# A new written order for the beginning of a two-layer cross-attention kernel: the second pair's context loaded and cast early, all values ahead of the first scores of group 1

## The chip, the cores and the metric

The kernel runs on one core of a Trainium2 chip. The metric is the device time of one execution in microseconds. Of the kernel before, three runs were timed: 1496.53, 1501.82 and 1505.2 us, median 1501.82. One further execution was profiled and took 1496.42 us.

## The reference

Two cross-attention layers follow each other over x, 16 sequences of 256 tokens and 320 channels, with a context of 16 x 256 tokens and 512 channels. There are 20 heads of 16 channels. Layer 0 takes the first 77 context tokens as text and the other 179 as image tokens; layer 1 takes the last 4 as image tokens. In short, for layer 0:

```
q, k, v   = x @ Wq, text @ Wk, text @ Wv          (k_ip, v_ip from the image tokens)
text_out  = softmax(q k / 4) v                    per head
text_probs= softmax((q . k_text over all channels) / 4)
sem       = (text_probs @ text) . image / 4       one number per query and image token
ip_out    = softmax(q k_ip / 4 + sem / 2) * spatial_mask @ v_ip
x         = (text_out + ip_out) @ Wout + bout + x
```

Layer 1 has the same shape, with the semantic part per head and normalised. All is float32.

## The kernel before

**Precision.** Most products are made of float32r parts: a tensor is cast to a high half on ScalarE (`nc.scalar.copy`), and its low half is the difference, made on VectorE or POOL (`tensor_sub`). `cast(hi, lo, src)` (L231) issues the ScalarE part at once and returns a function that issues the low half on a given engine (L237); `halves` (L157, L160) does both. A product is then hi*hi + hi*lo + lo*hi.

**Layer 0.** Work goes by sequence b and by group g of four heads: 5 groups a sequence, 80 slots of layer 0, then 80 of layer 1. Sequences are taken in pairs c for the context: `keys0(c)` loads four context blocks of 128 channels x 512 tokens (256 KB each), casts them, and makes six key products, text and image for each of three blocks m of 128 key rows (the third has 64). Keys and queries go out to device memory and come back as stacks of heads (`stacks0`: parts K, Q, T, M), with rows appended for the semantic term and for the maxima. `values0_(b)` makes the values of one sequence in three steps of 12 matmuls (L246 by way of `prod`). `semantic0` makes the text probabilities, `tokens0` the token products M.

**A slot.** `slot0(k)` makes, in this order, the transposed maxima of group k+1 (`maxima0`, L694 to L699: two matmuls, a copy to `mt`, two small DMAs into the query stack), the plain scores of group k+2 for their maxima (`score0`, L686, reduced on VectorE at L687 and L688; it holds the one tile `whole`, two banks), the transposed scores and exponentials of its own group (`turned0`, L711 to L717), and the attention of the group before (`attend0`, L754). Between these, `fill` runs background steps: keys, queries, semantic parts, values, output products. Each background task has a list of times in slots; `fill(now)` runs all steps whose time has come, earliest first. `FIRST["k0"]` is this list for the second pair's keys: step 1 loads, steps 2 to 5 cast one block each, steps 6 to 11 are the six key products.

**Order.** TensorE runs in written order everywhere. In `begin` and `end` the other engines and their queues do too. In the slots between, a planner orders them by its own model of time, and `queued` and `anchor` add order dependencies (no semaphores) that keep a background instruction behind the slot's own on its engine. Each engine runs its instructions strictly in the order that results.

**The beginning (`begin`).** It does by hand what the tasks do later, for the first pair: it clears tiles, loads contexts, weights and the first two x, makes the text keys as blocks arrive (`key_terms`, L1416) with a few matmuls without use between them (`warm`, L730), then queries of sequence 0 (L1472), image keys, semantic parts, values of sequences 0 and 1, and the scores of groups 0 and 1. Raw loads lie in tiles that are used later for something else: `craw` (context) in the two `rawc` and the two `raw` tiles, `wkr` and `wkir` (key weights) in the four `P` tiles, `wvir` (image value weights) in `craw` again. The context tiles `ct` of pair 0 are the tiles that pair 1 takes next, so pair 1's casts come only after the last value and token product of pair 0. In slot 0 and its second half seven further `warm` matmuls each stand.

Lines that the prediction names: L83 any load or store issued by SP; L246 and L256 products of keys, values and tokens (L256 the third key block); L552 and L555 query and output projections; L541 and L542 low halves of x on POOL; L608 to L615 semantic scores; L786 and L765 transposes.

## Time and profile before

| what | us |
|---|---|
| profiled execution | 1496.42 |
| its span, first to last instruction | 1494.6 |
| TensorE busy | 1426.0 (95%) |
| TensorE weight loads | 1148.6 (77%) |
| POOL busy | 1215.5 (81%) |
| VectorE busy | 1118.7 (75%) |
| ScalarE busy | 920.2 (62%) |
| slot 0 starts | 52.05 |
| slot 1, slot 2, slot 3 start | 58.05, 73.52, 85.92 |

The start of slot 0 is that of its plain scores (L686), the starts of the others those of their transposed maxima (L694) on TensorE. The times are counted from the first instruction. Matmuls are pipelined and their ends are modelled, so a row's end can lie a little behind the start of the next. The granted clock is that of TensorE: 1.00 is the full one, and 0.50 occurs. A row of the engines' timeline has start, length, engine and line, operation, tiles out<-in, shapes, count, and in brackets the idle time of the engine in front of it with what ended it. "ACTq" and "SPq" rows are DMA issues by ScalarE's and SP's sequencers.

### The profile page before, as it was taken

How to read it: one execution, taken by the hardware profiler on the slowest of the kernel's cores; microseconds unless marked ns; L12 is line 12 of the kernel's file. 1: busy time of each engine (PE TensorE's matmuls, PEld its weight loads, DVE VectorE, ACT ScalarE, POOL GpSimd, SP SyncE). 2: the span in 40 equal slices, each digit the busy share in tenths (PEclk: the TensorE clock that was granted, in tenths of full speed). 3: DMA queues.
4: the chain of work that ended last, by engine and by line, in shares of the span. 5: the costliest groups of instructions: out<-in, count | busy, mean ns of one | idle time of the engine just before them, and what ended most of it. 6: DMA issues, size and time to landing. Idle time of an engine off the chain costs nothing.

```text
span 1494.6 us, 36273 instructions
## 1 busy us (share of the span) xinstructions
PE 1426.0 (95%) x12738; PEld 1148.6 (77%) x12738; DVE 1118.7 (75%) x2527; ACT 920.2 (62%) x2174; POOL 1215.5 (81%) x1589
## 2 busy tenths in 40 slices
PE   8999999999999989789999999999999999999998
PEld 6877888888888877577777777777777777777765
DVE  6476767676777688767777887778777877787886
ACT  5455555556565655546676676667666766676663
POOL 6379898989898978788687888888888888888785
PEclk9999999999999999889999999999999999999999
DMA  7758676767677766575434434444444344433401
GB/s 246 226 178 239 173 230 192 215 197 223 198 218 204 205 191 176 157 221 166 132 94 120 141 117 116 120 142 117 112 127 140 113 121 128 138 109 93 122 26 47
DMA packets 228673, 232.83 MB, mean 156 GB/s; under 512 B 38346, under 2 KB 198380, under 8 KB 228492
## 3 DMA queue, kind: packets, MB, share of 16 engines
q1 hardware_dynamic: 226284, 229.21, 53.4%
q8 instruction: 102, 1.67, 0.5%
q10 hardware_dynamic: 2208, 1.30, 0.4%
q14 instruction: 79, 0.65, 0.1%
HBM read 117.65 MB, written 77.07 MB: 130 GB/s over the span
## 4 chain that ended last, share of the span: by engine, by line
PE 67%; DVE 9%; POOL 9%; DMA 8%; ACT 4%; issue 3%; SPq 1%; ACTq 1%; DVEq 0%; POOLq 0%
PE X L896 13%; PE X L246 12%; PE X L552 6%; PE P L754 5%; PE S L686 5%; PE P L908 4%; PE P L918 4%; PE T L711 3%; POOL wt L887 3%; PE T L846 3%; PE S L852 3%; POOL P L717 2%; PE X L555 2%; PE X L256 2%; PE X L511 2%
## 5 line engine op out<-in xcount | busy, mean ns | idle before, releaser
L717 POOL TENSOR_TENSOR P<-P,rs 128x512 f32<-128x512 f32 x320 | 406.6, 1293 | 87.7 <-ACT P L714 86.0
L887 POOL TENSOR_TENSOR wt<-P,ctb 128x512 f32<-128x512 f32 x316 | 400.5, 1289 | 50.6 <-ACT ctb L886 50.6
L896 PE MATMUL X<-ctb,gm 128*128 128x512 f32 x1106 | 298.3, 401 | 2.6 <-DVE wt L897 2.6
L714 ACT ACTIVATE P<-T 128x512 f32<-128x512 f32 x320 | 176.0, 594 | 139.8 <-PE T L711 104.4
L897 DVE TENSOR_TENSOR wt<-X,wt 128x512 f32<-128x512 f32 x320 | 216.9, 681 | 57.6 <-PE X L896 52.4
L866 ACT ACTIVATE P<-T 128x512 f32<-128x512 f32 x320 | 174.4, 592 | 81.1 <-PE T L846 77.3
L896 PEld LDWEIGHTS X<-ctb,gm 128*128 128x128 f32 x1106 | 192.2, 189 | 41.2 <-DVE wt L897 12.1
L854 DVE TENSOR_REDUCE mn<-S 128x4 fp32r<-128x1008 f32 x160 | 191.1, 1195 | 0.0
L886 ACT ACTIVATE ctb<-P 128x512 fp32r<-128x512 f32 x316 | 181.1, 625 | 9.0 <-PE X L896 6.1
L688 DVE TENSOR_REDUCE mn<-S 128x4 fp32r<-128x716 f32 x160 | 142.4, 890 | 0.0
L754 PE MATMUL P<-P,vr 128*32 128x256 f32 x1920 | 124.8, 388 | 2.0 <-POOL P L717 2.0
L686 PE MATMUL S<-ks,qs 125*128 125x256 f32 x640 | 116.3, 304 | 5.8 <-DMA ks<-kd 2.6
L686 PEld LDWEIGHTS S<-ks,qs 125*128 125x128 f32 x640 | 87.4, 192 | 40.2 <-issue 26.8
L711 PE MATMUL T<-qs,ks 127*128 127x256 f32 x640 | 105.6, 287 | 1.2 <-ACT P L714 0.9
L687 DVE TENSOR_REDUCE mn<-S 128x4 fp32r<-128x308 f32 x160 | 74.6, 466 | 25.0 <-PE S L686 23.7
L711 PEld LDWEIGHTS T<-qs,ks 127*128 127x128 f32 x640 | 89.2, 192 | 3.1 <-ACT P L714 1.9
L754 PEld LDWEIGHTS P<-P,vr 128*32 128x32 f32 x1920 | 55.6, 111 | 43.1 <-POOL P L717 4.3
L765 DVE STREAM_TRANSPOSE nt<-P 128x512 f32<-128x512 f32 x80 | 56.8, 710 | 42.2 <-PE P L754 40.9
L918 PE MATMUL P<-wt,zone 128*32 128x256 f32 x1280 | 85.4, 379 | 0.6 <-DVE wt L897 0.6
L908 PE MATMUL P<-P,v1t 128*32 128x256 f32 x1280 | 85.7, 385 | 0.0
L246 PE MATMUL X<-wC,cta 128*128 128x324 f32 (+1 forms) x480 | 79.7, 313 | 0.3 <-DVE kst L268 0.3
L846 PEld LDWEIGHTS T<-qs,ks 50*128 50x128 f32 x640 | 49.3, 185 | 39.3 <-issue 30.5
(382 smaller groups left out, 3042.3 us busy)
## 6 DMA issues: line engine op xcount, KB each, us to landing
qd<-q SPq DMA_DIRECT2D x96, 256.0 KB
qs<-tph SPq DMA_DIRECT2D x64, 308.0 KB
rawc<-in_cT_dram SPq DMA_DIRECT2D x60, 256.0 KB
qs<-qd SPq DMA_DIRECT2D x80, 192.0 KB
ks<-kd SPq DMA_DIRECT2D x80, 192.0 KB
ks<-kd SPq DMA_DIRECT2D x160, 96.0 KB
qs<-qd SPq DMA_DIRECT2D x160, 96.0 KB
kd<-kst SPq DMA_DIRECT2D x57, 256.0 KB
```

Of the source, the lines that this page charges most:

```text
L246: last = mm(out, lhs(a, k), rhs(b, k), start=i == 0, stop=i == len(terms) - 1)
L686: mm(sp[:, h], Q[: XROW + T0, h, t * 128 : (t + 1) * 128], K[: XROW + T0, h], start=True, stop=True)
L711: mm(st[p][:, j], K[:KS0, 2 * p + j, t * 128 : (t + 1) * 128], Q[:KS0, 2 * p + j], start=True, stop=True)
L714: exp = anchor(nc.scalar.activation(pt, st[p], AF.Exp, scale=SCALE))
L717: anchor(nc.gpsimd.tensor_mul(pt, pt, rs[:, t : t + 1].to_broadcast([128, 2, S])))
L754: mm(pv[32 * s : 32 * s + 32, o : o + S], v[:, vt, h : h + 32], P[k, s // 2][:, t, s % 2], start=vt < 2, stop=vt != 1,)
L854: anchor(nc.vector.tensor_reduce(maxes[k + 2][:, t], sp[:, :, :T1], axis=AX.X, op=ALU.max))
L866: anchor(nc.scalar.activation(P[k, u][:, t], st[u], AF.Exp, scale=SCALE))
L886: nc.scalar.activation(R[k, u][:, t], P[k, u][:, t], AF.Copy, scale=0.5)
L887: anchor(nc.gpsimd.tensor_sub(W[k, u][:, t], P[k, u][:, t], f(R[k, u][:, t])))
L896: mm(yp, gm[:, gb], R[k, u][:, kt], start=i == 0, stop=i == len(blocks[n]) - 1)
L897: w1["wt"] = nc.vector.tensor_mul(W[k, u][:, n], yp, W[k, u][:, n])
```

## The change

In `begin`:
- the loads of `wk` go out on ScalarE's DMA queue, `tmask` is loaded after x0, and the copy of the identity stands behind these;
- the three value tiles are cleared on POOL, behind its other clears, and the six additions of `tmask` to their ones column are ScalarE activations later on;
- low halves of the key weights and of all three query weight blocks are made on VectorE, those of the image key weights all on POOL, their four casts together;
- the image value weights are loaded into the `P` tiles instead of `craw`, so `craw` is free after the text keys, and the second pair's context is loaded into it at once (`step(("k0", 1))`);
- all of `v0` (three steps) stands ahead of `score0(0, 0)`, all of `v1` around `score0(0, 1)` and ahead of `score0(1, 0)`; the four casts of the second pair's context (`parts(k1, ...)`) stand around the two halves of `score0(1, ...)`;
- the two calls of `maxima0` issue their DMAs from ScalarE, their default, instead of SP;
- step 5 of sequence 1's queries stands after the last image value weights.

The times of the second pair's six key products change from 1.2, 1.6, 1.6, 2, 2.2, 2.6 to 0.2, 0.6, 1, 1.2, 1.6, 2 slots. In `begin`, `queued` adds no dependency.

```diff
-    anchors = {}
+    anchors, written = {}, [True]
     def queued(inst, *behind):
+        if written:
+            return inst
...
-    FIRST = {"k0": [-1, 0.2, 0.6, 0.6, 1, 1.2, 1.6, 1.6, 2, 2.2, 2.6], "s0": [-1, -1, -1, -1, -1, 0.2, 0.6]}
+    FIRST = {"k0": [-1, -1, -1, -1, -1, 0.2, 0.6, 1, 1.2, 1.6, 2], "s0": [-1, -1, -1, -1, -1, 0.2, 0.6]}
...
-        nc.scalar.copy(ident_r, ident)
...
-        dma(tmask, tmask_d)
         for k in range(4):
             dma(craw[k], cT_d[k * 128 : (k + 1) * 128, : 2 * S])
-            dma(wkr[k], rows(wk0_d, k))
+            nc.scalar.dma_start(wkr[k], rows(wk0_d, k))
         dma(x0, by_tile(xT_d[0]))
+        dma(tmask, tmask_d)
+        nc.scalar.copy(ident_r, ident)
...
-        for v in vr:
-            V.memset(v, 0.0)
-            V.memset(vcols(v, V0W)[:, 2, :, 16], 1.0)
-            for t in range(2):
-                V.tensor_scalar_add(vcols(v, V0W)[:, t, :, 16], vcols(v, V0W)[:, t, :, 16], tmask[:, t : t + 1])
...
             P.memset(f(ks[i])[:, :, :T0], 0.0)
+        for v in vr:
+            P.memset(v, 0.0)
+            P.memset(vcols(v, V0W)[:, 2, :, 16], 1.0)
...
             low(V)
-            loww(P)
+            loww(V)
...
+        wvir = [b[:, :320] for b in both]
         for k in range(4):
-            wvir = craw[k][:, :320]
-            dma(wvir, rows(wvi0_d, k))
+            dma(wvir[k], rows(wvi0_d, k))
...
-        lowq[0](V)
-        lowq[2](P)
+        for v in vr:
+            for t in range(2):
+                to = vcols(v, V0W)[:, t, :, 16]
+                nc.scalar.activation(to, to, AF.Identity, bias=tmask[:, t : t + 1])
+        for low in lowq:
+            low(V)
         V.tensor_scalar_mul(wqt[:, 2, CH : 2 * CH], f(wqt[:, 2, CH : 2 * CH]), tmask[:, 3:4])
-        lowq[1](V)
         dma(nts[0][:, :320], rows(wv0_d, 3))
+        step(("k0", 1))
...
+        lowi = []
         for m in range(3):
             key_evac(0, m, text[m])
+        for k in range(4):
+            lowi.append(cast(*rounded(wkit[k]), wkir[k]))
+        lowi[0](P)
+        lowi[1](P)
+        for m in range(3):
             n = 64 if m == 2 else 128
             P.tensor_copy(kt[:n, m, :, :, :T0], f(kst[m][:n, :, :, :T0]))
-        lowi = [cast(*rounded(wkit[k]), wkir[k]) for k in range(2)]
-        lowi[0](V)
-        lowi[1](P)
+        lowi[2](P)
+        lowi[3](P)
...
         lowi[0](V)
         lowi[1](P)
-        parts(q1)
...
         lowi[0](V)
         lowi[1](P)
+        parts(q1)
         get(*m1)
-        v0 = ("v0", 0)
-        parts(v0)
+        v0, k1 = ("v0", 0), ("k0", 1)
+        get(*v0)
         score0(0, 0)
...
-        parts(v0)
+        parts(v1)
         score0(0, 1)
+        get(*q1)
+        parts(v1, v1)
+        maxima0(0)
         stacks0(2)
-        get(*v0)
-        get(*q1)
-        maxima0(0, nc.sync)
+        get(*v1)
         parts(s1, s1, s1)
-        parts(v1)
+        parts(k1, k1)
         score0(1, 0)
-        parts(v1)
+        parts(k1)
         score0(1, 1)
         stacks0(3)
-        get(*v1)
-        maxima0(1, nc.sync)
-        parts(s1, s1, ("k0", 1))
+        parts(k1)
+        maxima0(1)
+        parts(s1, s1)
```

More of the change, by code (lines that the diff above doesn't have):

```diff
@@ L1483, in begin @@
             key_terms(1, m, 0, image_keys[m])
-        lowi = [cast(*rounded(wkit[k]), wkir[k]) for k in range(2, 4)]
-        lowi[0](P)
-        lowi[1](P)
         qd = dram.tile([3, CH, S], F32, tag="qd0", name="qd0", bufs=2)
@@ L1531, in begin @@
         lowv[1](P)
-        lowi = [cast(wvit[k // 2][:, 0, k % 2], wvit[k // 2][:, 1, k % 2], craw[k][:, :320]) for k in range(2)]
+        lowi = [cast(wvit[k // 2][:, 0, k % 2], wvit[k // 2][:, 1, k % 2], wvir[k]) for k in range(2)]
         stacks0(1, "QTK")
@@ L1542, in begin @@
             results[s0] = e.value
-        lowi = [cast(wvit[k // 2][:, 0, k % 2], wvit[k // 2][:, 1, k % 2], craw[k][:, :320]) for k in range(2, 4)]
+        lowi = [cast(wvit[k // 2][:, 0, k % 2], wvit[k // 2][:, 1, k % 2], wvir[k]) for k in range(2, 4)]
         lowi[0](V)
         lowi[1](P)
+        parts(q1)
         get(*m1)
-        v0 = ("v0", 0)
-        parts(v0)
+        v0, k1 = ("v0", 0), ("k0", 1)
+        get(*v0)
         score0(0, 0)
@@ L1574, in xattn2 @@
         begin()
+        written.clear()
     with tc.manual_schedule(engines=PINNED):
```

## The prediction

> **What bounds the kernel now.** I read three views in this order: busy time by stretches of the first 86 us, the chain of work that ended last, then the engines' timelines at each place where the chain changes engine. The stretches are cut where the stages change: text keys of the first pair; queries, semantic part and image keys; the stretch to the first scores (L686); from there to slot 0; and slots 0, 1 and 2. Columns after the length are busy us of PE, PEld, DVE, ACT and POOL, granted clock, DMA share, GB/s.
>
> ```profile
> 0.00:16.30 16.30, 12.45 (x50) 9.39 (x51) 11.59 (x31) 8.68 (x18) 10.95 (x30) 0.81 0.86 285
> 16.30:30.20 13.90, 13.14 (x95) 12.29 (x94) 7.85 (x24) 9.63 (x31) 8.41 (x17) 0.98 0.70 216
> 30.20:37.38 7.18, 4.39 (x34) 3.96 (x34) 3.35 (x9) 3.96 (x12) 3.83 (x6) 1.00 0.79 217
> 37.38:52.05 14.67, 14.12 (x93) 13.84 (x93) 6.38 (x14) 3.35 (x10) 0.00 (x0) 0.88 0.84 250
> 52.05:58.05 6.00, 6.00 (x36) 5.20 (x37) 3.21 (x8) 4.23 (x13) 3.83 (x3) 1.00 0.81 224
> 58.05:73.52 15.47, 12.52 (x101) 10.75 (x98) 8.54 (x16) 7.16 (x16) 9.64 (x11) 1.00 0.71 197
> 73.52:85.92 12.40, 10.70 (x97) 9.44 (x95) 9.68 (x22) 6.26 (x16) 6.08 (x6) 1.00 0.73 229
> ```
>
> TensorE is busy for nearly all of 37.38 to 58.05; the loose stretches are the start, 30.20 to 37.38, and slot 1 (2.95 us idle of 15.47). All that the change can win in its own stretch lies in these 86 us; the rest of the program keeps its written order. The chain (start, us, what) says why:
>
> ```profile
> 7.19 1.09 DVE cta L237
> ...
> 30.65 3.10 DMA kd<-ho
> 33.88 3.37 DMA ks<-kd
> 37.38 1.20 PE S L686 x4
> ...
> 49.13 0.48 PE S L686 x4
> 49.60 1.77 PE X L246 x12
> ```
>
> The first low half (L237) starts at 7.19 because VectorE clears the value tiles first; the first scores wait for keys that go out to memory and back (3.10 + 3.37 us); from there TensorE runs through values of 1.77 us each, with the scores between them.
>
> **The start: memsets off VectorE, key weights on ScalarE's queue.**
>
> ```profile
> 2.00 0.95 DVE L1399 MEMSET vr<- 128x1068 f32 x1 [0.17 <-issue]
> ...
> 12.59 0.74 DVE L237 TENSOR_TENSOR wE<-nt,wE 128x260 fp32r<-128x260 f32 x3
> ```
> ```profile
> 1.82 1.25 POOL L1407 MEMSET ks<- 128x308 f32 x4
> ```
> ```profile
> 4.53 0.62 ACT L231 CAST cta<-rawc 128x512 fp32r<-128x512 f32 x1 [2.21 <-DMA rawc<-in_cT_dram]
> ...
> 9.31 0.62 ACT L231 CAST ctb<-craw 128x512 fp32r<-128x512 f32 x1 [0.18 <-DMA craw<-in_cT_dram]
> ```
> ```profile
> 11.00:12.00 1.00, 1.00 (x4) 0.81 (x4) 0.40 (x1) 1.00 (x3) 1.00 (x3) 0.50 1.08 399
> ...
> 18.00:19.00 1.00, 1.00 (x11) 1.00 (x10) 1.00 (x2) 0.00 (x0) 1.00 (x2) 1.00 0.27 87
> ```
>
> Three memsets of 0.95 us leave VectorE and become POOL's: at the 1.25/4 us that POOL takes for 308 columns, 1068 columns are about 1.08 us each, so POOL is done near 6.5 us and waits for nothing but the later image weights. The low half of block 0 can follow its cast at about 5.1 instead of 7.19: 2.1 us. Against this VectorE now also makes the low halves of the key weights (0.74 a block, four blocks), and the four blocks still arrive as before, the last cast at 9.31: its two low halves (0.69 by the row of L160 below, and 0.74) end near 11.4, and TensorE ends the text keys near 13 to 14 instead of 16.29. The DMA engines are full here (share 1.08 at 399 GB/s), so a second issuing queue brings little; four issues ahead of ScalarE's first cast take what the earlier start gives. I take 2.0 us earlier for everything up to the image keys, between 0 (the stream of loads and VectorE decide) and 3.3.
>
> The early load of the second pair's context, four times 256 KB, or 2.6 us at 399 GB/s, stands in SP's queue behind the last value weights and ahead of the query stores. Its cover is the hole at 18 to 20 us (share 0.27 at 18). Without that cover it costs up to 2.6 us on the query store and then on the keys, which is a rival below. I take 0. The six additions that move to ScalarE as activations, tmask's later place and the separate tiles for the image value weights come out as 0 by the same rows: ScalarE is idle for 7.6 of the first 16.30 us.
>
> **From the image keys to slot 0.**
>
> ```profile
> 33.54 1.22 POOL L237 TENSOR_TENSOR wD<-craw,wD 128x320 fp32r<-128x320 f32 x1 [0.89 <-ACT wD L231]
> ```
> ```profile
> 44.77 0.24 DVE L611 TENSOR_TENSOR sp<-sp,X 128x77 f32<-128x77 f32 x1 [1.59 <-ACT sp L610]
> ...
> 45.98 0.15 DVE L615 TENSOR_SCALAR mx<-mx 128x1 f32<-128x1 f32 x1
> 47.40 0.48 DVE L687 TENSOR_REDUCE mn<-S 128x4 fp32r<-128x308 f32 x1 [1.26 <-PE S L686]
> 47.79 0.89 DVE L688 TENSOR_REDUCE mn<-S 128x4 fp32r<-128x716 f32 x1
> ...
> 62.36 0.69 DVE L160 TENSOR_TENSOR ctb<-raw,ctb 128x512 fp32r<-128x512 f32 x1
> ```
> ```profile
> 43.99 0.35 ACT L696 CAST mt<-X 8x256 fp32r<-8x256 f32 x1
> ```
> ```profile
> 63.66 1.85 ACTq L699 DMA_DIRECT2D qs<-mt  x2
> ```
>
> "All values ahead of slot 0" was so already; what is new is that they all come ahead of score (1,0), three of them ahead of score (0,0). The last low half that these need (wD) ends at 34.76 now and at 32.8 then; two values of 1.77 follow, and score (0,0) can start at 36.3, with its keys landed at about 35.3. So 2.6 us of idle in front of L686 are filled, and with them the half clock that follows: 0.88 over 14.67 us is 1.76 us of lost clock. Then 0.48 + 1.77 + 0.48 + 2 x 1.77 bring TensorE to 42.6 with nothing left to lay over what comes next, which is the same work as before in a worse order. The maxima's copy starts at 42.8. From it to the first small addition of the semantic part it is 0.78 us (43.99 to 44.77); now the pair of maxima DMAs stands between them on ScalarE, 1.85 us, because they are issued there and not on SP. Queued behind them on ScalarE are the semantic copies and all four casts; VectorE waits for these. So the small additions start at 45.4 and end 1.36 later (44.77 to 46.13), at 46.8; two low halves of 0.69 follow, to 48.2; only then comes the reduction of score (1,0), 1.28 for its two parts, to 49.5. Score (1,1) has to wait for it, since there is one bank pair for plain scores. One more low half and the next reduction bring 51.4, the transposed maxima 51.6, and slot 0 starts at 51.7 instead of 52.05: **-0.35 us**. Of the 2.0 at the start, the 2.6 and the 1.76, some 6 us go into this tail, in which TensorE waits 4.8 us from 44.7 to 49.5. If ScalarE and VectorE got to the reductions at once, slot 0 would start at 45.2 (-6.8); if the start gains nothing, at 53.7 (+1.65).
>
> After such a wait the clock is low again. 2.58 us of idle cost 1.76 us in the stretch from 37.38; here part of the half-clocked time lies over the second wait, so I put half of it on slot 0: **+0.9**, between 0 and 3.4.
>
> **Slots 0 to 2.** Six key products move forward: three into slot 0, one stays in slot 1, the last two come there from slot 2.
>
> ```profile
> 59.18 0.58 PE L246 MATMUL X<-cta,wA 128*128 128x156 f32 x4
> ...
> 63.10 0.45 PE L246 MATMUL X<-ctb,wA 128*128 128x156 f32 x2 [0.39 <-DVE ctb L160]
> ...
> 70.52 1.19 PE L552 MATMUL X<-hq,wE 128*128 128x256 f32 x7 [0.96 <-POOL hq L541]
> ```
> ```profile
> 82.46 0.76 PE L246 MATMUL X<-cta 128*77 128x192 f32 x6 [1.36 <-DVE q L160]
> ```
> ```profile
> 71.72 1.97 PE X L246 x12
> ...
> 74.81 0.86 PE X L256 x8
> ```
>
> An image product is 1.97, a text product 1.29 (0.86 for 8 matmuls, 12 of them); the last block has 0.86 and 1.31. Slot 0 gets 1.29 + 1.97 + 1.29 = **+4.55**, and its warm-up matmuls stay, so nothing there hides them. Slot 1 loses these 4.55 and the waits inside the first product (63.55 - 59.18 - 1.29 = 3.08) and gets 0.86 + 1.31 = 2.17. But the query product then comes too early: it is held until POOL's low half hq, 3.26 of products plus 0.96 of wait now, 4.22; with 0.86 of products ahead the wait is 3.36, 2.40 more. Slot 1: **-3.06**. Slot 2 loses 2.17 and perhaps its wait of 1.36, since one bank fewer is in the ring there; I take half, **-2.87**, between -0.8 (the work only covered a wait) and -3.5. The three: -1.38.
>
> The sum: -0.35 + 0.9 - 1.38 = -0.8 us. The profiled execution took 1496.42, so 1495.6; it lies 5.4 under the median of the runs shown, which puts the forecast at 1501.0 as a median.
>
> A rule of the Trainium skill bears on the clock term (TensorE: Matmul & The Clock Gate, section "What's actually happening"): the half clock is the default, and only about 3.4 us of sustained activity releases it. The trace agrees as far as it goes, with 0.88 behind a wait of 2.58; by the rule the term would be nearer 3.4 than 0.9, if slot 0 has to earn a whole busy window.
>
> **The rivals.**
> - *The tail is hidden.* ScalarE gets its casts done in the waits before 42 us, or the reductions go first; then -6.8, no clock term, -1.38: 1493.6. For it: ScalarE is busy 3.35 of 14.67 us there. Against: each engine works in its written order, and the casts overwrite the context tiles that the last value still reads. Chance 0.22.
> - *The early load pushes the keys* (the one on the slower side). If the 1 MB has no hole, query stores and keys leave 2.6 us later than now: first scores at 40.0 instead of 36.3 (+3.7), plus a half-clocked stretch of 1.76. With -0.8 that is +4.7: 1506.5. It decides once keys land after 36.3. For it: 399 GB/s in the stream until 18. Against: 87 GB/s just behind it. Chance 0.14.
> - *The clock.* Slot 0 runs through two half-clocked stretches like the one behind 37.38 (1.76 us each) instead of half of one: 3.5 for 0.9, +2.6, 1503.6. For it: the wait is nearly twice that of 2.58. Against: the second wait takes part of it. Chance 0.10.
> - *The order far behind is redrawn.* From slot 0 on, the engines other than TensorE are ordered by a planner, and a shift at the start can change that order. Single waits of this kind stand late in layer 0:
>
> ```profile
> PE X L694 <- DVE mn L688: 10.9, 10, 4.9
> PE X L627 <- ACT sp L623: 6.3, 1, 6.3
> ```
>
> One more or less of both (4.9 + 6.3) is -11 or +11: 1490 or 1512. Chance 0.12, both ways alike.
>
> **How the numbers follow.** The forecast holds 0.42, with its own range 1497 to 1505. Its bounds together with the hidden tail and the early load give 1493 to 1507; to leave no more than 2 in 10 outside I add part of the redrawn order and the 0.6% by which the runs shown differ: 1487 to 1511. About 0.5%, 7.5 us, can be told from no change. Faster by more: 0.15 of the hidden tail, 0.06 of the order, 0.04 of the forecast, 0.25. Slower by more: 0.06 of the early load, 0.03 of the clock, 0.06 of the order, 0.01 of the forecast, 0.16. The rest, 0.59, is no change.
>
> **What would show it.** Right: the first low half near 5, text keys ending near 13 to 14, score (0,0) with no wait in front near 36, then one long TensorE wait in front of score (1,1), ended by VectorE's reduction, and slot 0 near 51.7; in slot 1 no waits inside key products but over 3 us in front of L552 for hq. Wrong: slot 0 before 47; L686 still waiting for ks; a slot 1 of 15 us; or a first 86 us that shortens by what the total does not show.

## The result, and the profile after

The changed kernel takes 1511.68 us (median of 6 runs, 1508.18 to 1518.67), the kernel before 1499.07 us beside it (6 runs, 1492.34 to 1505.2). The ratio is 1.0089, with a 95% interval of 1.0067 to 1.0111: 0.9% slower. The prediction was 1501.0 us and no change; 1511.68 lies just above the range, which ended at 1511. The profiled execution took 1508.18 us with a span of 1506.3, so 11.7 us more span than before. Of all executions timed below, one was slow (of y4, 2215.67 us at a granted clock of 0.556), and the ratios leave it out.

Busy time by stretches of the changed kernel, cut at the same events as before, except that the fourth stretch begins at 37.96 us, 0.47 us behind the start of the first scores (columns after the length: busy us of PE, PEld, DVE, ACT and POOL, granted clock, DMA share, GB/s):

```profile
0.00:15.26 15.26, 13.38 (x50) 10.27 (x51) 9.28 (x33) 9.85 (x24) 5.66 (x20) 1.00 0.91 310
15.26:28.90 13.64, 12.92 (x96) 12.04 (x93) 6.49 (x22) 9.72 (x32) 9.62 (x20) 1.00 0.85 265
28.90:37.96 9.06, 8.20 (x61) 7.97 (x62) 3.41 (x8) 4.94 (x13) 3.77 (x6) 1.00 0.78 227
37.96:58.17 20.21, 9.53 (x68) 8.79 (x66) 8.31 (x18) 4.16 (x10) 0.00 (x0) 0.76 0.86 236
58.17:70.57 12.40, 12.40 (x74) 11.48 (x73) 4.29 (x10) 5.43 (x15) 5.66 (x6) 0.83 0.15 39
70.57:84.69 14.12, 11.13 (x81) 9.63 (x81) 5.80 (x13) 4.91 (x12) 8.16 (x9) 0.81 0.62 206
84.69:96.19 11.50, 9.00 (x80) 7.87 (x79) 9.41 (x19) 5.36 (x13) 5.78 (x5) 0.94 0.56 142
```

| event | before, us | after, us | difference |
|---|---|---|---|
| text keys done | 16.29 | 15.26 | -1.0 |
| first scores (`score0(0, 0)`) | 37.38 | 37.49 | +0.1 |
| slot 0 starts | 52.05 | 58.17 | +6.1 |
| slot 3 starts | 85.92 | 96.19 | +10.3 |
| end of the span | 1494.6 | 1506.3 | +11.7 |

Three things are to be seen. The start gains a microsecond, and the first scores do not. Between them and slot 0 the time goes from 14.67 to 20.7 us (37.49 to 58.17), and in the last 20.2 of these TensorE is busy for 9.53 only. Slots 0 to 2 take 38.0 us for 33.9, at a granted clock of 0.81 to 0.94 where it was 1.00. Behind slot 3 only 1.4 us are added.

The 1.00 in the first row is no measurement: the clock records of this execution begin at 14.5 us. The rows say more. Eight matmuls of the text keys in the changed kernel, then the same eight in x2 (below), whose order is the same up to slot 0:

```profile
11.45 1.83 PE L1416 MATMUL X<-ctb,wA 128*128 128x156 f32 x8
```
```profile
9.09 1.02 PE L1416 MATMUL X<-ctb,wA 128*128 128x156 f32 x8
```

TensorE ran its text keys slowly here until about 14 us, as in the kernel before, where the same eight take 1.83 us at a granted clock of 0.50. In x2 they end at 11.46 instead of 15.26 us, and the first scores come no earlier for it (37.37).

**From the first scores to slot 0.** TensorE's timeline of the changed kernel (start, length, what, and in brackets the idle time in front and what ended it):

```profile
37.49 0.72 PE L688 MATMUL S<-ks,qs 125*128 125x256 f32 x4 [0.47 <-DMA ks<-kd]
...
45.27 0.67 PE L688 MATMUL S<-ks,qs 125*128 125x256 f32 x4
55.35 1.23 PE L688 MATMUL S<-ks,qs 125*128 125x256 f32 x4 [9.40 <-DVE mn L690]
```

The plain scores stand at L688 now. Those of the second half of group 1 wait 9.40 us for VectorE's reduction. VectorE's timeline, and ScalarE's, of the same stretch:

```profile
51.58 0.24 DVE L613 TENSOR_TENSOR sp<-sp,X 128x77 f32<-128x77 f32 x1 [9.81 <-ACT sp L612]
...
52.80 1.30 DVE L162 TENSOR_TENSOR cta<-rawc,cta 128x512 fp32r<-128x512 f32 x2
54.01 0.47 DVE L689 TENSOR_REDUCE mn<-S 128x4 fp32r<-128x308 f32 x1
```
```profile
44.33 0.35 ACT L698 CAST mt<-X 8x256 fp32r<-8x256 f32 x1
48.30 2.99 ACTq L701 DMA_DIRECT2D qs<-mt  x2
51.32 0.35 ACT L612 COPY sp<-X 128x77 f32<-128x77 f32 x2 [6.64 <-DMA qs<-mt]
51.56 1.15 ACT L159 CAST cta<-rawc 128x512 fp32r<-128x512 f32 x2
```

Read backwards: the reduction stands behind two low halves and the small additions, the additions wait 9.81 us for ScalarE's copy `sp`, and that copy stands behind the two DMA issues of the maxima. Their source `mt` is ready at 44.68, but the first issue starts at 48.30 and the second ends at 51.3. The view of `mt` has their own lengths (shortest, middle, longest, in ns):

```profile
L701 ACTq DMA_DIRECT2D qs<-mt x2: 601/918/1234, 48.3 to 50.7; - x2
```

So the issues themselves take 1.23 and 0.60 us, 1.83 together. The other 4.77 of the 6.64 us of idle time are two waits, 3.62 and 1.15 us, and some 0.04 us at the end. In the records each of the two waits for the completion count of a load that SP issued shortly before and that uses the same semaphore. SP's rows:

```profile
44.66 0.59 SPq L83 DMA_DIRECT2D ks<-kd  x1
...
45.80 0.90 SPq L83 DMA_DIRECT2D qs<-tph  x1
```

The last count of the first comes at 48.22, and the issue starts at 48.30; that of the second comes at 50.66, and the issue starts at 50.68. The Trainium skill (DMA: Bandwidth & Descriptors, section "Anatomy of one DMA — SWDGE (gpsimd) path") says that a wait for a semaphore takes place on the issuing sequencer, ahead of the dispatch, and not in the DMA engines; the trace agrees, and shows that all of ScalarE stands still for it, 4.77 of the 6.64 us here.

**The clock.** Stretches of 2 us of the changed kernel, with the granted clock third from the end:

```profile
48.00:50.00 2.00, 0.00 (x0) 0.00 (x0) 0.00 (x0) 0.00 (x0) 0.00 (x0) 0.66 0.76 209
50.00:52.00 2.00, 0.00 (x0) 0.00 (x0) 0.38 (x2) 0.68 (x3) 0.00 (x0) 0.50 0.97 222
...
60.00:62.00 2.00, 2.00 (x7) 1.61 (x6) 0.90 (x3) 2.00 (x8) 0.74 (x1) 0.50 0.01 3
62.00:64.00 2.00, 2.00 (x16) 1.78 (x15) 0.42 (x1) 0.53 (x2) 1.78 (x2) 0.93 0.00 0
```

From 48.6 us on the clock is 0.50, through the wait and through the first 4 us of slot 0, until 62.3. The next changes in the clock records are at 79.3, 86.2 and 103.2 us; all these steps are multiples of 3.41 us.

**Slots 1 and 2.** TensorE's timeline, then VectorE's:

```profile
77.83 0.39 PE L554 MATMUL X<-hq,wE 128*128 128x256 f32 x1 [0.58 <-ACT hq L541]
80.63 1.86 PE L554 MATMUL X<-hq,wE 128*128 128x256 f32 x7 [2.41 <-POOL hq L543]
82.29 1.40 PE L258 MATMUL X<-cta,wB 128*128 128x360 f32 x4
...
94.32 1.16 PE L248 MATMUL X<-wC,cta 128*128 128x320 f32 x6 [2.50 <-DVE q L162]
```
```profile
90.55 2.32 DVE L162 TENSOR_TENSOR wF<-rawc,wF 128x256 fp32r<-128x256 f32 x2
92.79 0.41 DVE L773 TENSOR_TENSOR tmp<-nt,P 128x256 f32<-128x256 f32 x1
93.12 0.81 DVE L162 TENSOR_TENSOR wF<-rawc,wF 128x256 fp32r<-128x256 f32 x2
93.86 0.41 DVE L162 TENSOR_TENSOR q<-X,q 128x256 fp32r<-128x256 f32 x1
```

The query product waits 0.58 + 2.41 us for `hq`, and is followed by half clock (0.50 from 80 to 86 us; a half of L258's product takes 1.40 us here). Slot 2 waits 2.50 for `q`, whose low half stands on VectorE behind the low halves of the output weights `wF`. Both waits stood in slots 1 and 2 before, at 0.96 and 1.36 us.

### The profile page after: what moved, and what is told of

It is laid out like the page before. It is cut to its first block, busy times and chain, and to the rows that moved or that the text cites. A ratio compares the mean times of both kernels' runs of the same rounds, so it can differ in the third digit from the quotient of the medians.

```text
span 1506.3 us, 36279 instructions
## 1 busy us (share of the span) xinstructions
PE 1431.4 (95%) x12738; PEld 1154.1 (77%) x12738; DVE 1119.2 (74%) x2527; ACT 923.0 (61%) x2180; POOL 1211.8 (80%) x1583
## 4 chain that ended last, share of the span: by engine, by line
PE 71%; DMA 8%; POOL 7%; DVE 6%; ACT 3%; issue 3%; SPq 2%; ACTq 1%; DVEq 0%; POOLq 0%
PE X L898 13%; PE X L248 12%; PE P L756 6%; PE X L554 6%; PE S L688 5%; PE P L910 4%; PE T L713 4%; PE P L920 4%; PE T L848 3%; PE S L854 3%; POOL wt L889 3%; POOL P L719 2%; PE X L258 2%; SPq L83 2%; PE X L513 2%
## 5 line engine op out<-in xcount | busy, mean ns | idle before, releaser
L889 POOL TENSOR_TENSOR wt<-P,ctb 128x512 f32<-128x512 f32 x316 | 401.4, 1293 | 48.9 <-ACT ctb L888 48.6
L688 PE MATMUL S<-ks,qs 125*128 125x256 f32 x640 | 117.6, 307 | 12.1 <-DVE mn L690 11.5
L688 PEld LDWEIGHTS S<-ks,qs 125*128 125x128 f32 x640 | 88.6, 194 | 46.7 <-issue 21.9
L713 PE MATMUL T<-qs,ks 127*128 127x256 f32 x640 | 107.0, 290 | 0.6 <-ACT P L716 0.5
L713 PEld LDWEIGHTS T<-qs,ks 127*128 127x128 f32 x640 | 90.7, 195 | 2.4 <-ACT P L716 1.6
```

The costliest lines, as they stand in the source:

```text
L688: mm(sp[:, h], Q[: XROW + T0, h, t * 128 : (t + 1) * 128], K[: XROW + T0, h], start=True, stop=True)
L713: mm(st[p][:, j], K[:KS0, 2 * p + j, t * 128 : (t + 1) * 128], Q[:KS0, 2 * p + j], start=True, stop=True)
L889: anchor(nc.gpsimd.tensor_sub(W[k, u][:, t], P[k, u][:, t], f(R[k, u][:, t])))
```

## The experiments

Theory at the start: the loss has three parts, ScalarE's hold, the early load in front of the keys, and the early key products. The rival: one cause, the half clock behind the one long wait, and the rest is its echo. The table gives, for every profiled execution, the start of the first scores (L686 or L688), that of the transposed scores (L711 or L713) of slot 0, and the time from there to slot 5, all from TensorE's timelines; then median, ratio to the kernel before on the same chip, and its 95% interval. The kernel before had medians of 1498.8 to 1501.3 us beside the different groups, so medians are compared within a group (x, y, z, w) and ratios across them. A single execution's places shift by a microsecond or two with the clock; the ratio is what decides. All the edits stand ahead of slot 5. From there to the end the profiled executions take 1390 to 1398 us, and these 8 us do not follow the edits, so the first 100 us explain a ratio only in part.

| kernel | first scores | slot 0 | slots 0 to 5 | median us | ratio | interval |
|---|---|---|---|---|---|---|
| before | 37.38 | 52.60 | 47.1 | 1499.07 | 1 | |
| after | 37.49 | 59.16 | 53.5 | 1511.68 | 1.0089 | 1.0067 to 1.0111 |
| x1 | 38.58 | 58.20 | 48.9 | 1508.79 | 1.0056 | 1.0027 to 1.0085 |
| x2 | 37.37 | 58.89 | 44.9 | 1499.73 | 0.9989 | 0.9969 to 1.0009 |
| x3 | 37.48 | 52.45 | 49.3 | 1496.85 | 0.9980 | 0.9955 to 1.0006 |
| x4 | 35.74 | 50.97 | 48.5 | 1493.66 | 0.9959 | 0.9937 to 0.9982 |
| y1 | 38.57 | 54.88 | 53.6 | 1505.38 | 1.0024 | 1.0001 to 1.0047 |
| y2 | 38.16 | 53.43 | 46.3 | 1494.94 | 0.9965 | 0.9947 to 0.9982 |
| y3 | 34.35 | 51.12 | 46.6 | 1494.50 | 0.9964 | 0.9942 to 0.9987 |
| y4 | 34.62 | 52.52 | 45.9 | 1493.90 | 0.9969 | 0.9945 to 0.9993 |
| z1 | 37.80 | 52.59 | 50.4 | 1504.84 | 1.0034 | 1.0012 to 1.0055 |
| z2 | 37.42 | 54.22 | 48.6 | 1501.37 | 1.0010 | 0.9987 to 1.0034 |
| z3 | 38.24 | 56.70 | 46.3 | 1498.73 | 0.9995 | 0.9978 to 1.0013 |
| z4 | 34.46 | 51.63 | 47.0 | 1497.19 | 0.9998 | 0.9975 to 1.0021 |
| w1 | 37.36 | 52.58 | 49.4 | 1498.23 | 0.9991 | 0.9970 to 1.0013 |
| w2 | 36.76 | 53.02 | 44.7 | 1490.91 | 0.9953 | 0.9923 to 0.9983 |
| w3 | 37.73 | 54.03 | 46.3 | 1496.49 | 0.9983 | 0.9962 to 1.0004 |

All edits below are against the changed kernel.

**x1: the maxima's DMAs back on SP.**

```diff
-        maxima0(0)
+        maxima0(0, nc.sync)
...
-        maxima0(1)
+        maxima0(1, nc.sync)
```

> The changed kernel with one edit: both maxima DMAs of the beginning are issued by SP again, not by ScalarE. Theory A (ScalarE's queue is held, 44.68 to 51.3, by these two issues, which wait until DMAs issued by SP just before have landed; everything written behind them waits along): the semantic copies start near 45.2 instead of 51.3, score (1,1) near 48.5 to 50 instead of 55.35, slot 0 near 51.5 to 53 instead of 58.17, total about 5 to 6 us under the changed kernel. Rival B (VectorE's low halves in front of the reductions make the wait by themselves): score (1,1) not before 53, total less than 2 us under the changed kernel.

TensorE's timeline of x1:

```profile
52.25 0.73 PE L688 MATMUL S<-ks,qs 125*128 125x256 f32 x4 [3.00 <-DVE mn L690]
...
57.21 1.19 PE L688 MATMUL S<-ks,qs 125*128 125x256 f32 x4 [2.57 <-DMA ks<-M]
```

The wait for VectorE falls from 9.40 to 3.00 us, so ScalarE's hold was two thirds of it; rival B falls with it. The gain at slot 0 is 1 us only, not the 5 to 6 that theory A asked for: slot 0 now waits for `ks<-M`, which SP issues behind the maxima. Slots 0 to 5 take 4.6 us less, though nothing in them was changed; the wait of 2.41 us for `hq` is still there, but no half clock follows it in this execution. The ratio falls by 0.33%, some 5 us, with overlapping intervals, and does not reach that of before.

**x2: the key products at their old times**, the new tail left as it is.

```diff
-    FIRST = {"k0": [-1, -1, -1, -1, -1, 0.2, 0.6, 1, 1.2, 1.6, 2], ...
+    FIRST = {"k0": [-1, -1, -1, -1, -1, 1.2, 1.6, 1.6, 2, 2.2, 2.6], ...
```

> The changed kernel with one edit: the six key products of the second pair keep the times of before (1.2, 1.6, 1.6, 2, 2.2, 2.6 slots); load and casts stay early. Theory A (products moved into slot 0 cost their full length there and only uncover the wait for POOL's low half hq in slot 1): slots 0 to 2 take about 36 us instead of 38.0, slot 1 waits less than 1.5 us in front of the query product, total 1 to 3 us under the changed kernel. Rival B (the longer slots come from the half clock behind the long wait alone): slots 0 to 2 take 37.5 to 38.5, total the same. Slot 0 still starts near 58.2 in both.

Slot 0 comes as late as in the changed kernel (58.89), but slots 0 to 5 take 44.9 us for 53.5, and the ratio falls from 1.0089 to 0.9989, by some 15 us where 1 to 3 were expected. Two losses, then, and the larger one lies behind slot 0: the rival of one cause falls. This run also repeats ScalarE's hold:

```profile
46.98 0.35 ACT L698 CAST mt<-X 8x256 fp32r<-8x256 f32 x1
48.09 2.94 ACTq L701 DMA_DIRECT2D qs<-mt  x2
51.06 0.35 ACT L612 COPY sp<-X 128x77 f32<-128x77 f32 x2 [3.73 <-DMA qs<-tph]
```

The source `mt` is ready 2.65 us later than in the changed kernel, SP's two loads land at the same times within 0.3 us (48.01 and 50.40), and ScalarE goes on at the same time within 0.3 us: it is SP's loads that set the end of the hold, not the maxima.

**x3 and x4: the old tail with the new start**, with the early load of the second pair's context (x3), and without it (x4, load and casts where they were before). Both have the old times.

```diff
-        get(*v0)
+        parts(v0)
         score0(0, 0)
...   the tail of the kernel before, to the end of begin
```
```diff
-        step(("k0", 1))
...   x4 alone, beside the old tail
-        parts(s1, s1)
+        parts(s1, s1, ("k0", 1))
```

> The changed kernel with the end of its beginning in the order of before (values between the scores, maxima DMAs by SP, casts of the second pair in slots 0 and 1 at the old times); the new start and the early load stay. Theory A (the loss is made in the new order of the tail): slot 0 starts at 50.5 to 52.5, slot 1 loses the 2 us of waits for context that lands late, total 0 to 4 us under the kernel before. Rival B (the early load makes keys and later loads late): the first scores wait longer for keys than in the changed kernel (37.5), slot 0 after 53, total over the kernel before.

> As the kernel with the old order of the tail, and the second pair's context is also loaded at the old place, so that of the change only the new start is left. Theory A (the early megabyte takes DMA time from the query stores and token rows and so eats what the start gains): key stores leave sooner, the first scores start at 36 to 36.5 instead of 37.5, slot 0 near 50.5 to 51.2. Rival B (keys' way through memory has its own latency, whatever else moves): first scores at 37.2 to 37.6 as in both kernels so far. Total 0 to 2 us under the kernel before in either case, slot 1 with the old waits for late context.

TensorE's timeline of x3, then of x4:

```profile
37.48 1.19 PE L688 MATMUL S<-ks,qs 125*128 125x256 f32 x4 [5.55 <-DMA ks<-kd]
```
```profile
35.74 1.19 PE L688 MATMUL S<-ks,qs 125*128 125x256 f32 x4 [4.68 <-DMA ks<-kd]
```

The early load makes the keys 1.74 us later in this pair. All the runs together say it more safely: in the eleven with the early load at its place the first scores wait for the keys until 36.76 to 38.58 us, in the four where it stands later and the keys are waited for (x4, y3, y4, z4) until 34.35 to 35.74. The means differ by 2.9 us. Without the load the new start alone is worth 0.4% (x4). Where these 6 us are won is not shown: in the profiled executions slot 5 of x4 starts at 99.5 us, that of before at 99.7.

**y1 to y4.** The maxima on POOL's queue, which is idle from 38 us to slot 0, free ScalarE without burdening SP (y1); y2 adds the old times of the products to it; y4 also moves the early load behind the stacks of group 1. y3 keeps only the new order of the values: old load and casts of the second pair, old times, maxima on SP.

```diff
-        maxima0(0)
+        maxima0(0, nc.gpsimd)
...   the same for maxima0(1): y1; with the old times: y2
```
```diff
-        step(("k0", 1))
...
         stacks0(1, "QTK")
+        step(("k0", 1))
...   y4, beside y2's edits
```
```diff
-        parts(k1, k1)
         score0(1, 0)
-        parts(k1)
         score0(1, 1)
         stacks0(3)
-        parts(k1)
...   y3, beside SP for the maxima, old FIRST, no early step
```

> The two maxima DMAs go out on POOL's queue, where nothing stands from 38 us to slot 0; nothing else of the changed kernel is touched. Theory A (ScalarE's queue is held at the two issues): the copies of the semantic part follow the copy of the maxima at once, the small additions start near 45.4, score (1,1) near 50 after a wait of 3 to 5 us, slot 0's scores near 52.5 instead of 58.17; the later part stays as it is, so 1511.7 - 5.5 = about 1506, ratio to before 1.003 to 1.006. Theory B (the issues cost ScalarE little; it is the order of VectorE, casts' low halves ahead of the reduction, that sets it): score (1,1) stays at 54 to 55, slot 0 at 57 to 58, ratio 1.009.

> The same, with the six key products at their old times. If the hold of ScalarE's queue and the early products are two separate losses that add (5.5 us and 12 us): slot 0's scores near 52.5, slot 3 near 84.6 (32.1 us later, as with the old times alone), 1499.7 - 5.5 = about 1494, ratio 0.995 to 0.998. If the first gain is given back in slots 0 to 2 (hq, low halves on VectorE and landings set their ends): slot 0 near 52.5 but slot 3 near 88 to 90 and ratio 0.999 as with the old times alone.

> Of the new tail only the order of the values is left: all of v0 ahead of score (0,0), all of v1 ahead of score (1,0); the second pair's context is loaded and cast where it was, its products have their old times, the maxima go out on SP. Theory A (values first is harmless by itself; the casts and ScalarE's issues make the tail): score (1,1) waits under 2 us for VectorE, slot 0's scores at 46 to 50.4, no later than with the old tail (50.44). Theory B (values first leaves nothing to lay over the reductions): a wait of 3 us or more in front of score (1,1), slot 0 at 52 to 55, ratio 1.000 or more.

> Maxima on POOL's queue, old times of the products, and the early load of the second pair's context behind the stacks of group 1 on SP's queue instead of ahead of the query stores. If the early load is what delays the keys (1.74 us between the two kernels with the old tail): first scores at 35.7 to 36 instead of 37.4, slot 0 about 1.5 us earlier than in the run with the early load. Theory of no effect: first scores stay at 37.4. Against a gain: the casts have to wait for the load, which now shares the DMA engines with the stacks; then the wait in front of score (1,1) grows by that. Ratio 0.994 to 0.998, about 1 to 2 us under the run with the early load.

The timeline of y1, on POOL and on ScalarE, then on TensorE:

```profile
46.94 0.34 ACT L698 CAST mt<-X 8x256 fp32r<-8x256 f32 x1
47.46 0.23 ACT L612 COPY sp<-X 128x77 f32<-128x77 f32 x1 [0.18 <-PE X L610]
47.60 1.32 POOL L701 DMA_DIRECT2D qs<-mt  x2 [16.19 <-ACT mt L698]
...
51.56 0.74 PE L688 MATMUL S<-ks,qs 125*128 125x256 f32 x4 [3.01 <-DVE mn L690]
```

ScalarE goes on 0.18 us behind the copy of the maxima, and on POOL, whose DMAs carry semaphores of their own in the records, both issues take 1.32 us and wait for nothing but the copy. Slot 0 comes 4.3 us earlier than in the changed kernel, and the ratio is 1.0024 for 1.0089: theory A. (The ratio's fall, some 10 us, is more than the 4.3; slots 0 to 5 are as long as in the changed kernel, so the rest is not accounted for.) A wait of 3.01 us stays in front of the second scores of group 1, in y1, y2, y4 and the z kernels with early casts alike; in y3, which has no casts there, it is 1.78. So VectorE's order costs 3 us, of which the casts' low halves are 1.2.

y2: the two gains add, as the first of the two expectations had it. y3 says that values first by itself costs nothing that can be told from x4; its first scores come at 34.35, earliest of all. y4 against y2: the load's later place brings the first scores forward by 3.5 us, but slot 0 by only 0.9. TensorE's timeline of y4:

```profile
46.09 1.04 PE L688 MATMUL S<-ks,qs 125*128 125x256 f32 x4 [3.01 <-DVE mn L690]
...
51.53 1.19 PE L688 MATMUL S<-ks,qs 125*128 125x256 f32 x4 [2.75 <-DMA ks<-M]
```

What is won goes into a wait for the rows M of group 2. Medians and intervals of y2, y3, y4 and x4 cannot be told apart.

**z3 and z4: can that wait be ordered away?** The rows T and M of groups 2 and 3 go out ahead of the load (z3, on y4) or simply earlier (z4, on y3 with POOL's queue).

```diff
         stacks0(1, "QTK")
+        stacks0(2, "TM")
+        stacks0(3, "TM")
...
-        stacks0(2)
+        stacks0(2, "KQ")
...
-        stacks0(3)
+        stacks0(3, "KQ")
```

> The kernel with maxima on POOL's queue, old product times and the load of the second pair's context behind the stacks of group 1; now the rows T and M of the stacks of groups 2 and 3 stand ahead of that load on SP's queue, since slot 0 waited 2.75 us there for M. If that wait is only a matter of the queue's order: slot 0's scores at 48.8 instead of 51.5, total 1491 to 1492, ratio 0.994. If the DMA engines are the limit (the same bytes, and the keys of group 2 land no earlier): slot 0 waits for ks<-kd or the maxima instead, slot 0 at 50.5 to 51.5, total as before, 1493 to 1494.

> The kernel that keeps only the new order of the values (old load and casts of the second pair, old product times), with the maxima on POOL's queue and the same rows T and M early. Slot 0 waited 2.66 us there for M. Queue order: slot 0's scores at 47.5 instead of 50.1, slot 3 about 2 us earlier (it then waits for the late casts again), total 1491 to 1493. DMA engines as the limit: slot 0 near 50, total 1494 as before.

TensorE's timeline of z3, and two stretches of it:

```profile
55.71 1.19 PE L688 MATMUL S<-ks,qs 125*128 125x256 f32 x4 [3.17 <-DMA qs<-qd]
```
```profile
44.00:48.00 4.00, 2.64 (x23) 2.38 (x21) 2.05 (x8) 2.68 (x8) 1.32 (x2) 1.00 1.05 370
48.00:52.00 4.00, 1.33 (x5) 0.94 (x5) 3.28 (x6) 0.56 (x2) 0.00 (x0) 0.50 0.98 326
```

No. The beginning of this execution of z3 was late (its first scores come at 38.24 without a wait for keys), so the plain scores of slot 0 are counted from the first scores: 17.5 us in z3 for 16.9 in y4, 16.2 in z4 for 15.8 in y3. In z3 slot 0 waits for another part of the same stacks, with a DMA share of 1.05 and 0.98. That speaks for the transfers themselves as the limit, but SP also issues almost without a break from 43.4 to 52.6 us there, and no run separates the two. In z4 slot 0 has a wait of 3.60 us that the profile puts down to no DMA. Both medians are even higher than those of y4 and y3 (by 4.8 and 2.7 us, with overlapping intervals), which was not expected and is not explained.

**z1 and z2: what do the early products cost?** The theory calls a product the cover of a wait when TensorE works on it while another engine finishes what comes next. With POOL's queue they cost 10.4 us (y1 to y2). z1 moves the sixth product ahead of the query product that waits for `hq`; z2 leaves one product at the end of slot 0 and puts five into slot 1, all ahead of that query product.

```diff
-    FIRST = {"k0": [-1, -1, -1, -1, -1, 0.2, 0.6, 1, 1.2, 1.6, 2], ...
+    FIRST = {"k0": [-1, -1, -1, -1, -1, 0.2, 0.6, 1, 1.2, 1.5, 1.55], ...   z1
+    FIRST = {"k0": [-1, -1, -1, -1, -1, 1, 1.2, 1.2, 1.5, 1.5, 1.55], ...   z2
```

> The changed kernel with its maxima on POOL's queue (1505.4 us) and its early key products, but the sixth product stands in slot 1 ahead of the first query products, which wait 0.58 + 2.41 us for hq in that run, instead of behind them: this product is even earlier than in the change. Theory A (what the early products cost is cover: a wait for hq, and half clock behind it): the wait for hq falls to 1.4 us or less, the half clock of 76 to 83 us is gone or shorter, and slot 3 starts 1.5 to 4 us earlier relative to slot 0 than the 37.6 us of that run (34 to 36); total about 1502. Theory B (a product costs the more, the earlier it is made, by itself): slot 0 to slot 3 stays at 37.6 or more, total 1505 or more.

> The same with one product in the last part of slot 0 and five in slot 1, all ahead of the first query products. Theory A (cover): no wait for hq, no half clock in slot 1, slot 0 about 2 us longer than with the old times (7.3 + 1.3), slot 0 to slot 3 between 32.5 and 34.5 us (33.1 with the old times, 37.6 with those of the change); the wait of 1.4 to 1.7 us for q in slot 2 stays. Total 1495 to 1498. Theory B (early products cost by themselves): between the two, near 35.5, total 1500.

Half right. Slots 0 to 3 take 35.9 us in z1 and 32.9 in z2 (y1 37.6, y2 33.1), the half clock of slot 1 is gone in both, and z2 does not wait for `hq` at all; z1 still waits 1.95 us for it, where 1.4 or less was expected. But z1's total is that of y1 (ratio 1.0034 and 1.0024), and z2's ratio stays 0.45% above y2's, with the intervals just apart. In both the wait for `q` in slot 2 has grown to 2.5 us (y1 1.66, y2 1.37), and one of 1.9 for the reduction stands behind slot 3, as in y1 (y2 0.58), with half clock behind one or the other. Covering one wait uncovered the next.

**w1, w2 and w3: who is behind the next wait?** VectorE makes low halves of `wF` ahead of both. The task that loads and casts these weights comes one slot later, with the early products (w1, against y1), with z2's times (w2) and with the old times (w3, against y2).

```diff
-    task(("w4", 0), [2.6, 2.8, 3, 3.2], ...
+    task(("w4", 0), [3.6, 3.8, 4, 4.2], ...
```

> Maxima on POOL's queue and the early products of the change; the loads and casts of the output weights (task w4, its low halves wF stand on VectorE ahead of q in slot 2 and ahead of the reduction in slot 3) come one slot later, at 3.6 to 4.2. Theory A (the products were the cover of VectorE's work on wF): the wait for q in slot 2 falls from 1.7 to under 0.7 us, that of 1.9 us for the reduction in slot 3 is gone, and with it the half clock at 100 to 104 us; the wait for hq in slot 1 stays at 2.4 + 0.6. Slot 5 starts 4 to 5 us earlier relative to slot 0 (53.6 in the run with POOL's queue), total about 1500 to 1502. Theory B (other causes): the waits stay, or they only move by one slot with the weights; total 1504 or more.

> The same with one product at the end of slot 0 and five in slot 1. Theory A: neither hq nor q nor the reduction is waited for over 1 us in slots 1 to 3, slot 0 to slot 5 at 45 to 46.5 us (48.6 with the weights at their old time, 46.3 with the old product times); total 1495 to 1497 for 1501.4. Theory B: slot 0 to slot 5 stays near 48.6, or a wait of the same size stands a slot later; total 1500 or more.

> The same with the old product times, where the wait for q is 1.4 us. Theory A: that wait goes, slot 0 to slot 5 at 45 instead of 46.3, total 1493 to 1494 for 1494.9 (hardly to be told apart). Theory B, that the weights a slot later run into the next background work: 1496 or more.

TensorE's timeline of w1, all waits of slots 1 to 4:

```profile
71.28 0.38 PE L554 MATMUL X<-hq,wE 128*128 128x256 f32 x1 [0.58 <-ACT hq L541]
74.07 1.86 PE L554 MATMUL X<-hq,wE 128*128 128x256 f32 x7 [2.41 <-POOL hq L543]
...
94.58 1.50 PE L756 MATMUL P<-P,vr 128*32 128x256 f32 x24 [1.37 <-DVE tmp L773]
96.71 0.74 PE L688 MATMUL S<-ks,qs 125*128 125x256 f32 x4 [0.63 <-DVE mn L690]
```

The wait for `q` and that of 1.9 us for the reduction are gone, a smaller one (1.37 + 0.63) stands in slot 4, behind the weights' low halves at their new place; the one for `hq` is as it was. So the waits moved with the weights, as theory B has it, but they also shrank. The sum of TensorE's waits for VectorE of over 0.45 us in slots 2 to 4 goes from 3.5 us (y1) to 2.0 (w1), from 4.3 (z2) to 2.2 (w2), and from 2.0 (y2) to 3.1 (w3, which has a new one of 1.13 for the keys `kst`). The ratio follows: it falls by 0.57% for z2's times (1.0010 to 0.9953, intervals apart), by 0.33% for the change's (1.0024 to 0.9991, intervals that overlap) and not at all for the old times (0.9965 and 0.9983, overlapping; w3's total of 1496.49 is the one named for theory B). That fits theory A, by which the weights on VectorE cost something only where the products that lay over them are gone; only the step from z2 to w2 is clear of the noise. At 0.9953 w2 is faster than before and after; its six executions are four near 1490 and two near 1498 us, and its interval overlaps those of x4, y2, y3 and y4.

## Why the prediction was wrong, step by step

- **The start** (2.0 us, between 0 and 3.3): the first low half came at 5.51, near the 5.1 foretold, but the text keys ended at 15.26, not at 13 to 14: 1.0 us gained, within the bounds, in an execution whose TensorE was slow until about 14 us. In x1 and x2, with the same order up to there, they ended at 11.4 and 11.5, 4.8 us earlier than before and outside the bounds. The clock decides this, and the term did not count it. In neither case did the gain reach the first scores, which wait for the keys.
- **The early load at 0, covered by the hole at 18 to 20 us.** The hole was used and was too small. Two stretches of before, and of after:

```profile
18.00:20.00 2.00, 2.00 (x19) 2.00 (x18) 1.13 (x2) 0.00 (x0) 1.46 (x4) 1.00 0.16 50
22.00:24.00 2.00, 1.73 (x14) 1.47 (x13) 1.18 (x3) 1.97 (x6) 1.57 (x4) 1.00 0.89 291
```
```profile
18.00:20.00 2.00, 2.00 (x16) 2.00 (x15) 0.42 (x1) 0.74 (x3) 2.00 (x7) 1.00 0.81 299
22.00:24.00 2.00, 2.00 (x18) 2.00 (x17) 1.02 (x5) 0.94 (x4) 2.00 (x4) 1.00 1.01 306
```

  It takes about 0.5 of the 1 MB (249 GB/s more for 2 us); the rest pushes what comes behind. The step that failed is the term put at 0: it measured 1.74 us (x3 to x4) to 3.5 us (y2 to y4). The first scores came at 37.49, not 36.3, and still behind a wait for `ks` (0.47 us), one of the prediction's own signs of being wrong; all of the start's gain is gone there. This was the rival with 0.14, right in kind and about right in size (2.6).
- **The tail (-0.35).** The chain was the predicted one, link by link: maxima's issues, semantic copies, small additions, two low halves, reduction, score (1,1). One link failed: the pair of issues on ScalarE, taken as 1.85 us from a pair at 63.66 us of the kernel before. The issues took 1.83 us, so their price was right; the waits of 3.62 and 1.15 us in front of them, for SP's loads on the same semaphores, were put at nothing, and ScalarE was held 6.64 us. Additions at 51.58 for 45.4, slot 0 at 58.17 for 51.7. With that link taken out (y1), the wait in front of score (1,1) is 3.01 us; the forecast of 4.8 without its 1.85 is 2.95.
- **The clock (+0.9, between 0 and 3.4).** Slot 0 ran its first 4 us at half clock. It took 12.40 us for the 10.55 that its products make (6.00 + 4.55), so 1.85: within the bounds, twice the value taken. The rule of the Trainium skill that the prediction weighed (TensorE: Matmul & The Clock Gate, section "What's actually happening") has the clock released after about 3.4 us of busy time; here TensorE is busy from 57.96 and the clock is full at 62.3, so it is a little over 4 us. The prediction read this rule as a cost near 3.4 us. But work goes on at half speed meanwhile: the kernel before lost 1.76 us that way, and slot 0 lost 1.85 us, somewhat under half of the time.
- **Slots 0 to 2 (-1.38).** They cost +4.15. Slot 0's products were right (+4.55, and the clock above). Slot 1 is 1.35 shorter for the predicted 3.06: its wait for `hq` was right (3.36 foretold, 2.99 measured), but not the half clock behind it, some 1.7 us. Slot 2 is 0.90 shorter for 2.87. Here the step failed that put half of the old wait of 1.36 to the credit ("one bank fewer is in the ring"; with that half, 0.68, the term is -2.85, not -2.87): the wait is for VectorE behind `wF`, and without the products that lay over it, it grew to 2.50. Besides, slot 2 begins at half clock (0.94 over the slot), which the term left out, so that TensorE's busy time fell by 1.70 and not by 2.17. The bound named for this case (-0.8, "the work only covered a wait") was right in kind; that its size fits so well is partly luck, since the half clock makes some 0.5 of it. That the cover is what was lost, w1 and w2 speak for; w3, with the old times, gained nothing.
- **The sum.** Against the profiled execution: +6.1 up to slot 0 for the predicted -0.35; +4.15 in slots 0 to 2 for -0.48 (with the clock term); +1.4 behind for 0. Together +11.7 for -0.8. The first part is 6.45 more than taken: 4.8 of ScalarE's waits, and 1.2 by which the first scores came later than the foretold 36.3, which the early load makes; some 0.5 are left.
- **The rivals.** The hidden tail did not occur in the change; even in y2 and y4, where ScalarE is free, slot 0 starts at 51.5 or later, far from the 45.2 of that rival. Two half-clocked stretches came as the rival of the clock had them (1.85 in slot 0 and some 1.7, for 3.5 in all), the second in slot 1 and not in slot 0. The order far behind was not needed; that its 1512 comes so near the measured 1511.68 is luck, since 10.3 of the 11.7 us stand ahead of slot 3. Behind slot 3 the difference to before runs between +8.6 and +14.8 us from slot to slot and ends at +11.7; what moves it there was not tried.

## What to carry to other kernels

A DMA issue had no fixed price here: the pair took 1.83 us by itself, but on ScalarE each issue stood at its place in the engine's order until SP's last DMA on the same semaphore had landed, 4.77 us in all. It is safer on a queue with nothing urgent behind it, as POOL's was, and what SP has in flight at that time has to be counted. Before work is moved forward out of a stretch, list what each engine has to finish under it: it was the cover of POOL's `hq` and VectorE's `wF`, and taking it away turned a planned gain into a loss of some 10 us (y1 against y2), of which slots 0 to 5 show 7. The background work has to move with it: with one product in slot 0 and five in slot 1, and the weights a slot later, w2 has the lowest ratio of all the kernels run, though not by more than the noise.

## What the runs showed of the hardware that was not expected

- Two small DMA issues (4 rows of 1 KB each) held ScalarE for 6.64 us, 4.77 of them waiting for loads that SP had issued on the same two semaphores, and took 1.32 us on POOL in the same place.
- A wait of the same length is sometimes followed by the half clock and sometimes not: in the changed kernel 2.41 us for `hq` are followed by 5.5 us at 0.50, the 2.50 us for `q` in slot 2 by none at once, and in x1 the same 2.41 us by none. The Trainium skill (TensorE: Matmul & The Clock Gate, section "What's actually happening") gives a reason, that the window of activity runs freely and does not begin with the work. The clock records agree with it: their changes at 48.6, 62.3, 79.3, 86.2 and 103.2 us lie on one grid of 3.41 us, and the same wait for `hq` lies differently on the grid: it begins 1.1 us before a step in the changed kernel and 0.7 us before one in x1. How much idle time in a window it takes is not shown.
- Executions of one kernel differ by several microseconds, and the longer ones have the lower granted clock: those of z2 at 1494 to 1500 us have 0.985 to 0.986, those at 1503 to 1508 us 0.978 to 0.982. The profiled executions of z1 and z2 lie 6 and 7 us under their medians, so their times cannot be taken for the medians.
